# Kept activations, early residual loads and more buffers around two batch norms

## Chip, cores, metric

One core of a Trainium2 chip. The metric is the device time of one execution in microseconds (us). The record calls a run of one core slow when it is over 1.5% above the fastest of its kernel. The profile's own span is 1 to 3 us shorter than the timed runs, and single executions of one kernel differ by about 0.3%, mostly by where the first pass ends. So I read small differences not from whole times but from a point inside the profile: **E, the end of the last matmul of the second product**, and the time from E to the end of the span.

## The reference, cut

x has 128 batches of 128 nodes with 256 features. Four graph layers follow, each `x = x + layer(relu(layernorm(x)))`. Layers 0 to 2 are local to a batch. Layer 3 has two batch norms over all 16384 tokens:

```python
agg = einsum('nm,bmd->bnd', A_hat, features).reshape(-1, 256)
h   = relu(batchnorm(agg @ W1.T + b1))        # 512 wide: statistics over all tokens
out = batchnorm(h @ W2.T + b2)                # 256 wide: statistics over all tokens
return x3 + out                               # x3: the input of layer 3
```

Each batch norm needs every token before it can scale the first one. So there are three passes over the 32 groups of four batches: z = agg W1 + b1 (with x3 and z put aside), then O = relu(norm(z)) W2, then out = x3 + norm(O).

## The kernel before

z of a group is 1 MB, x3 and the output are 512 KB each. The first pass stores z and x3 to DRAM. O stays in SBUF (128 KB per partition). The parts concerned:

```python
        # end of the first pass, for a group g
        nc.gpsimd.dma_start(X3[g], xt)
        # ... z[:, j, :] = bw1T.T @ gT + b1, its bn_stats ...
        nc.sync.dma_start(Z[g], z)

    sc1, sh1 = bn_affine(stats1, FC, g1_c, be1_c, "bn1")     # the root runs on GpSimd
    # ... O[g] allocated ...
    with tc.tile_pool(name="passB", bufs=4) as wb:           # second product
        for g in range(NG):
            z = wb.tile([P, FC, T], FP, tag="z", name=f"zi_{g}")
            nc.sync.dma_start(z, Z[g])
            # relu(scale * z + shift) on ScalarE, 8 matmuls on TensorE,
            # bias and statistics on VectorE -> O[g], stats2

    sc2, sh2 = bn_affine(stats2, DC, g2_c, be2_c, "bn2")
    with tc.tile_pool(name="passC", bufs=3) as wc:           # last pass
        for g in range(NG):
            x3 = wc.tile([P, G, D], FP, tag="x3", name=f"x3i_{g}")
            nc.sync.dma_start(x3, X3[g])
            # O[g] scaled on ScalarE, turned by TensorE, added into x3 on VectorE
            nc.gpsimd.dma_start(out[g * G : (g + 1) * G].rearrange("b n d -> n b d"), x3)
```

Of the kernel before, what the change touches and what calls it, by code (L numbers as in the profile page):

```python
# [8 lines left out]
FP = mybir.dt.float32  # L9
# [13 lines left out]
def kernel(  # L23
# [25 lines left out]
):  # L49
    """Four pre-norm graph layers over x[b, n, d], node n on the partitions.  # L50

    Layers 0 to 2 and the first product of layer 3 are local to a batch and run
    as one pass over groups of G batches. Layer 3's two batch norms are over all
    tokens: its first product goes to DRAM with the residual, and comes back
    once its statistics are known; the second product stays on chip until its own
    statistics are.

    A mixing matrix A enters as A^T[m, n]. With activations h[m, d] as the
    stationary operand, the product is (A h)^T, which is what the next weight
    product contracts; so mixing also transposes. A (h W) is computed as (A h) W  # L60
    where A h is the smaller one.
    """
    nc = tc.nc
# [17 lines left out]
    def bank(shape, name):  # L81
        return psum.tile(shape, FP, tag="bank", name=name)
# [6 lines left out]
    adj_sb = const.tile([P, P], FP, name="adj_sb")  # L89
    nc.sync.dma_start(adj_sb, adj)  # L90

    passA = ExitStack()
# [44 lines left out]
    def inv_sqrt(dst, src, eps):  # L137
        """dst = 1 / sqrt(src + eps), a few numbers in each partition."""
        if eps:
            nc.vector.tensor_scalar(dst, src, eps, None, ALU.add)  # L140
            src = dst
        nc.gpsimd.tensor_tensor(dst, src, nhalf[:, : dst.shape[1]], ALU.pow)  # L142

    with tc.tile_pool(name="prep", bufs=1) as prep:

        def turned(dst, src, nr, name):
            """dst[p, c, r * P + q] = src[q, r, c * P + p]: the transpose of the
            matrix whose P-row blocks are src[:, r, :]."""
            ncol = src.shape[-1] // P
            for c in range(ncol):  # L150
                pt = bank([P, nr, P], f"{name}_{c}")
                for r in range(nr):
                    nc.tensor.transpose(pt[:, r, :], src[:, r, c * P : (c + 1) * P], ident)
                nc.vector.tensor_copy(dst[:, c, :].rearrange("p (r q) -> p r q", r=nr), pt)
# [4 lines left out]

        # layer 0: origin * adj and origin^T * adj, origin = adj where adj <= 0, else 1  # L160
        for dst, src, name in ((ainT, adjT, "fi"), (aoutT, adj_sb, "fo")):
# [23 lines left out]

        # layer 1: the causal mask over the adjacency, Wq Wk^T and Wv Wo
        nc.gpsimd.affine_select(
# [17 lines left out]

        # layer 2: adj * adj
        nc.vector.tensor_tensor(a2T, adjT, adjT, ALU.mult)

        # layer 3: D^-1/2 (adj + I) D^-1/2 and what is used transposed
        an = prep.tile([P, P], FP, name="an")  # L210
# [33 lines left out]
    def norm(g, layer):  # L244
        """relu(layernorm(x)) of a group."""
        xt = X[g]
        st = small.tile([P, G, 6], FP, tag="st", name=f"st{layer}_{g}")
        mv = small.tile([P, G, 2], FP, tag="mv", name=f"mv{layer}_{g}")
        for b in range(G):
            nc.vector.bn_stats(st[:, b, :], xt[:, b, :])  # L250
        for b in range(G):
            nc.vector.bn_aggr(mv[:, b, :], st[:, b, :])
        rs = small.tile([P, G], FP, tag="rs", name=f"rs{layer}_{g}")
        inv_sqrt(rs, mv[:, :, 1], LN_EPS)
        sh = small.tile([P, G], FP, tag="sh", name=f"sh{layer}_{g}")
        nc.vector.scalar_tensor_tensor(sh, mv[:, :, 0], -1.0, rs, ALU.mult, ALU.mult)  # L256
        h = w.tile([P, G, D], FP, tag="h", name=f"h{layer}_{g}", bufs=3)
        for b in range(G):
            nc.scalar.activation(  # L259
                h[:, b, :], xt[:, b, :], AF.Relu, bias=sh[:, b : b + 1], scale=rs[:, b : b + 1]  # L260
            )
        return h

    def mixed(dst, src, aT, name):
        """dst[d, c, (b n)] = (A src[:, b, :])^T, chunks c of P features."""
        for c in range(src.shape[-1] // P):
# [7 lines left out]
    def front(g):  # L274
        """Layers 0 and 1 of a group of batches, in X[g]."""
        if g + 1 < NG:
# [4 lines left out]
        gl = small.tile([P, G, 3], FP, tag="gl", name=f"gl_{g}")  # L281
        gs = w.tile([P, D], FP, tag="gs", name=f"gs_{g}")
        for b in range(G):
# [60 lines left out]
        for b in range(G):  # L344
            for c in range(DC):
# [3 lines left out]
                )  # L349
        p = w.tile([P, G, P], FP, tag="p", name=f"p_{g}")  # L350
        nc.vector.scalar_tensor_tensor(
# [14 lines left out]
        for b in range(G):  # L366
            nc.tensor.transpose(pp[:, b, :], p[:, b, :], ident)
        pT = w.tile([P, G, P], FP, tag="pT", name=f"pT_{g}")
        nc.vector.tensor_copy(pT, pp)
# [13 lines left out]
    def back(g):  # L383
        """Layer 2 of a group, and layer 3 as far as its first product."""
        xt = X[g]
# [14 lines left out]
        yield  # L400
        uT = w.tile([P, HC1, T], FP, tag="hT", name=f"uT_{g}", bufs=3)
        mixed(uT, u, a2T, f"pmu_{g}")
# [38 lines left out]
        yield  # L441
        z = w.tile([P, FC, T], FP, tag="hT", name=f"zo_{g}", bufs=3)
        for j in range(FC):
# [7 lines left out]
            nc.vector.bn_stats(stats1[:, j, g, :], z[:, j, :])  # L451
        nc.sync.dma_start(Z[g], z)
        yield

    def together(*parts):
        """Emit parts in turns, a stage of each at a time."""
        parts = list(parts)
        while parts:
            parts = [q for q in parts if next(q, parts) is not parts]
# [6 lines left out]
    def bn_affine(stats, nch, gam, bet, name):  # L466
        """The scale and shift of a batch norm, a channel in each partition."""
        mv = const.tile([P, nch, 2], FP, name=f"mv_{name}")
# [9 lines left out]

    # layer 3: relu of the first batch norm, the second product kept on chip
    sc1, sh1 = bn_affine(stats1, FC, g1_c, be1_c, "bn1")  # L480
    keep = ctx.enter_context(tc.tile_pool(name="keep", bufs=1))
    O = [keep.tile([P, DC, T], FP, name=f"o_{g}") for g in range(NG)]
    with tc.tile_pool(name="passB", bufs=4) as wb:
        for g in range(NG):
            z = wb.tile([P, FC, T], FP, tag="z", name=f"zi_{g}")
            nc.sync.dma_start(z, Z[g])
            for j in range(FC):
                nc.scalar.activation(  # L488
                    z[:, j, :], z[:, j, :], AF.Relu,
                    bias=sh1[:, j : j + 1], scale=sc1[:, j : j + 1],  # L490
                )
            for i in range(DC):
                po = bank([P, T], f"po_{g}_{i}")
                for j in range(FC):
                    nc.tensor.matmul(  # L495
                        po, bw2T[:, j, i * P : (i + 1) * P], z[:, j, :],
                        start=(j == 0), stop=(j == FC - 1),
                    )
                nc.vector.tensor_scalar(O[g][:, i, :], po, b2_c[:, i : i + 1], None, ALU.add)
                nc.vector.bn_stats(stats2[:, i, g, :], O[g][:, i, :])  # L500

    # the second batch norm, turned back to node rows, and the residual
    sc2, sh2 = bn_affine(stats2, DC, g2_c, be2_c, "bn2")
    with tc.tile_pool(name="passC", bufs=3) as wc:
        for g in range(NG):
            x3 = wc.tile([P, G, D], FP, tag="x3", name=f"x3i_{g}")
            nc.sync.dma_start(x3, X3[g])
            for i in range(DC):
                nc.scalar.activation(
                    O[g][:, i, :], O[g][:, i, :], AF.Identity,  # L510
                    bias=sh2[:, i : i + 1], scale=sc2[:, i : i + 1],
                )
            for q in range(G // 2):
                pt = bank([P, 2, D], f"pto_{g}_{q}")
                for r in range(2):
                    b = 2 * q + r
                    for i in range(DC):
                        nc.tensor.transpose(
                            pt[:, r, i * P : (i + 1) * P], O[g][:, i, b * P : (b + 1) * P], ident
                        )  # L520
                nc.vector.tensor_tensor(
                    x3[:, 2 * q : 2 * q + 2, :], pt, x3[:, 2 * q : 2 * q + 2, :], ALU.add
                )
            nc.gpsimd.dma_start(
                out[g * G : (g + 1) * G].rearrange("b n d -> n b d"), x3
            )

# [33 lines left out]
```

## Time and profile before

Median 3216.8 us (4 runs, 3216.28 to 3217.32).

| stretch (us) | what | TensorE busy | DMA share |
|---|---|---|---|
| 0 to 2857 | first pass | 94% between 60 and 2840 | 0.06 |
| 2857 to 2867.2 | first batch norm's scale and shift, first z load | 0 | 0.72 |
| 2867.2 to 3088.8 | second product | all of it | 0.40 |
| 3088.8 to 3096.5 | second batch norm's scale and shift | little | 0.54 |
| 3096.5 to 3216 | last pass | 46% | 0.80 |

A busy engine is the bound only where it leaves no holes: TensorE in the first three rows but for one hole, nothing in the last.

### The profile page before, as it was taken

How to read it: one execution, taken by the hardware profiler on the slowest of the kernel's cores; microseconds unless marked ns; L12 is line 12 of the kernel's file. 1: busy time of each engine (PE TensorE's matmuls, PEld its weight loads, DVE VectorE, ACT ScalarE, POOL GpSimd, SP SyncE). 2: the span in 40 equal slices, each digit the busy share in tenths (PEclk: the TensorE clock that was granted, in tenths of full speed). 3: DMA queues.
4: the chain of work that ended last, by engine and by line, in shares of the span. 5: the costliest groups of instructions: out<-in, count | busy, mean ns of one | idle time of the engine just before them, and what ended most of it. 6: DMA issues, size and time to landing. Idle time of an engine off the chain costs nothing.

```text
span 3215.9 us, 27252 instructions
## 1 busy us (share of the span) xinstructions
PE 2936.7 (91%) x10287; PEld 1781.6 (55%) x10287; DVE 1329.0 (41%) x3629; ACT 945.1 (29%) x1765; POOL 176.5 (5%) x204
## 2 busy tenths in 40 slices
PE   5999999999999999999999999999999999989973
PEld 3555655555555555555555555555555555544443
DVE  5433344444443443344444443443344444224443
ACT  2222233323223222233323223222233322134460
POOL 0000000000000000000000000000000000000011
PEclk8999999999999999999999999999999999989975
DMA  2000000000000000000000000000000000024457
GB/s 101 27 14 20 20 27 27 27 27 27 26 27 27 27 14 20 20 27 27 27 27 27 27 27 27 26 14 21 19 26 27 27 27 20 20 111 149 152 181 263
DMA packets 44438, 142.45 MB, mean 44 GB/s; under 512 B 3586, under 2 KB 22548, under 8 KB 36116
## 3 DMA queue, kind: packets, MB, share of 16 engines
q1 hardware_dynamic: 33248, 105.46, 9.3%
q0 software_dynamic: 9216, 33.56, 2.7%
q8 instruction: 80, 1.31, 0.2%
q10 hardware_dynamic: 1844, 1.71, 0.2%
q14 instruction: 50, 0.41, 0.0%
HBM read 73.61 MB, written 67.11 MB: 44 GB/s over the span
## 4 chain that ended last, share of the span: by engine, by line
PE 60%; DVE 20%; issue 9%; ACT 4%; DMA 3%; POOL 3%; POOLq 0%; DVEq 0%; ACTq 0%; SPq 0%
PE p L408 17%; PE p L423 14%; PE pu L395 7%; DVE st L250 4%; ACT h L259 4%; PE pmu L269 4%; PE pq L326 4%; PE pv L337 3%; DVE gs L285 3%; POOL rs L142 3%; DVE stats L451 2%; DMA x3i<-x 2%; PE ps L346 2%; PE py L375 2%; PE pm_in L298 2%
## 5 line engine op out<-in xcount | busy, mean ns | idle before, releaser
L408 PE MATMUL p<-uT,w 128*128 128x512 f32 x2048 | 913.1, 592 | 0.0
L408 PEld LDWEIGHTS p<-uT,w 128*128 128x128 f32 x2048 | 379.4, 190 | 412.5 <-issue 394.4
L423 PE MATMUL p<-w,h2T 128*128 128x256 f32 x2048 | 447.2, 379 | 0.0
L423 PEld LDWEIGHTS p<-w,h2T 128*128 128x128 f32 x2048 | 389.1, 190 | 66.6 <-issue 15.3
L259 ACT ACTIVATE h<-x,sh,rs 128x256 f32<-128x256 f32 x512 | 265.5, 589 | 354.6 <-DVE sh L256 337.7
L269 PE MATMUL pg<-ahT,h 128*128 128x128 f32 x512 | 124.2, 435 | 146.5 <-ACT h L259 146.5
L446 PE MATMUL pz<-gT,bw1T 128*128 128x512 f32 x512 | 246.0, 629 | 4.0 <-DVE gT L272 3.6
L415 ACT ACTIVATE h2T<-p 128x512 f32<-128x512 f32 x128 | 75.7, 592 | 571.0 <-PE p L408 571.0
L395 PE MATMUL pu<-w,mT 128*128 128x512 f32 x512 | 228.8, 600 | 14.0 <-DVE mT L272 14.0
L413 DVE TENSOR_SCALAR h2T<-p 128x512 f32<-128x512 f32 x128 | 88.3, 690 | 365.1 <-PE p L408 365.1
L495 PE MATMUL po<-zi,bw2T 128*128 128x512 f32 x512 | 221.6, 596 | 10.5 <-ACT zi L488 10.5
L432 DVE TENSOR_TENSOR x<-pr,x 128x512 f32<-128x512 f32 x64 | 43.7, 683 | 447.4 <-PE pr L431 447.4
L269 PEld LDWEIGHTS pg<-ahT,h 128*128 128x128 f32 x512 | 115.7, 317 | 173.1 <-ACT h L259 173.0
L427 ACT COPY s<-p 128x512 f32<-128x512 f32 x64 | 37.5, 586 | 567.6 <-PE p L423 567.6
L250 DVE BATCH_NORM_STATS2 st<-x 128x6 f32<-128x256 f32 x512 | 190.8, 413 | 4.2 <-DMA x<-in_x_dram 2.0
L142 POOL TENSOR_TENSOR rs<-rs,nhalf 128x4 f32<-128x4 f32 x128 | 129.8, 1014 | 1135.7 <-DVE rs L140 1135.7
L495 PEld LDWEIGHTS po<-zi,bw2T 128*128 128x128 f32 x512 | 97.8, 191 | 134.3 <-issue 112.9
L446 PEld LDWEIGHTS pz<-gT,bw1T 128*128 128x128 f32 x512 | 98.9, 203 | 129.1 <-issue 92.9
L285 DVE SCALAR_TENSOR_TENSOR gs<-h,gw 128x256 f32<-128x256 f32 x384 | 161.4, 420 | 15.9 <-ACT h L259 0.7
L395 PEld LDWEIGHTS pu<-w,mT 128*128 128x128 f32 x512 | 94.9, 190 | 127.5 <-issue 90.4
L299 DVE TENSOR_TENSOR m_in<-pm_in,eb 128x512 f32<-128x512 f32 x64 | 44.3, 692 | 234.9 <-PE pm_in L298 234.9
L488 ACT ACTIVATE zi<-zi,sh_bn,sc_bn 128x512 f32<-128x512 f32 x128 | 93.4, 802 | 118.4 <-DMA zi<-z 118.4
(116 smaller groups left out, 2931.5 us busy)
## 6 DMA issues: line engine op xcount, KB each, us to landing
z<-zo SPq DMA_DIRECT2D x32, 1024.0 KB, 3.9
zi<-z SPq DMA_DIRECT2D x32, 1024.0 KB, 4.8
x<-in_x_dram SPq DMA_DIRECT2D x32, 512.0 KB, 5.9
x<-x POOLq DMA_DIRECT2D x32, 512.0 KB, 3.0
x3i<-x SPq DMA_DIRECT2D x32, 512.0 KB, 5.1
out_dram<-x3i POOLq DMA_DIRECT2D x32, 512.0 KB, 4.6
w<-in_L_gnn_W_dram SPq DMA_DIRECT2D x1, 2048.0 KB, 11.6
bw<-in_L_gnn_W_dram ACTq DMA_DIRECT2D x2, 512.0 KB
```

The lines of the kernel that those rows point to most:

```text
L142: nc.gpsimd.tensor_tensor(dst, src, nhalf[:, : dst.shape[1]], ALU.pow)
L250: nc.vector.bn_stats(st[:, b, :], xt[:, b, :])
L259: nc.scalar.activation(h[:, b, :], xt[:, b, :], AF.Relu, bias=sh[:, b : b + 1], scale=rs[:, b : b + 1])
L269: nc.tensor.matmul(pm[:, b, :], src[:, b, c * P : (c + 1) * P], aT, start=True, stop=True)
L285: nc.vector.scalar_tensor_tensor(gs, h[:, b, :], 1.0, gw[:, i, :], ALU.mult, ALU.mult, accum_out=gl[:, b, i : i + 1],)
L326: nc.tensor.matmul(pq, m_qk[:, c, i * P : (i + 1) * P], hT[:, c, :], start=(c == 0), stop=(c == DC - 1),)
L337: nc.tensor.matmul(pv[:, r, :], hT[:, c, b * P : (b + 1) * P], w_vo[:, c, :], start=(c == 0), stop=(c == DC - 1),)
L395: nc.tensor.matmul(pu, mT[:, c, b * P : (b + 1) * P], w1[:, c, :], start=(c == 0), stop=(c == DC - 1),)
L408: nc.tensor.matmul(p2, w2[:, c, j * P : (j + 1) * P], uT[:, c, :], start=(c == 0), stop=(c == HC1 - 1),)
L423: nc.tensor.matmul(p3[:, r, :], h2T[:, j, b * P : (b + 1) * P], w3[:, j, :], start=(j == 0), stop=(j == HC2 - 1),)
L446: nc.tensor.matmul(pz, bw1T[:, c, j * P : (j + 1) * P], gT[:, c, :], start=(c == 0), stop=(c == DC - 1),)
L495: nc.tensor.matmul(po, bw2T[:, j, i * P : (i + 1) * P], z[:, j, :], start=(j == 0), stop=(j == FC - 1),)
```

## The change

Its intent is threefold. The second product begins with the three groups whose z was made last, which are kept in SBUF. Six x3 loads are made during the second product, and nine more into the space of the z buffers, so that 15 x3 buffers are in use instead of three. Loads go to GpSimd's queue, and the output leaves in half groups on SyncE's queue. To find room, some buffers of the first pass are halved. The core of the diff:

```diff
+    zp = zs.enter_context(tc.tile_pool(name="zp", bufs=3, side="right"))
+    KEPT = range(NG - 3, NG)
...
-        z = w.tile([P, FC, T], FP, tag="hT", name=f"zo_{g}", bufs=3)
+        z = ZT[g] = zp.tile([P, FC, T], FP, tag="z", name=f"zo_{g}")
...
-        nc.sync.dma_start(Z[g], z)
+        if g not in KEPT:
+            nc.sync.dma_start(Z[g], z)
...  (gs, p, pT: bufs=1; uT: bufs=2)
+    EARLY = 6
+    x3p = ctx.enter_context(tc.tile_pool(name="x3p", bufs=EARLY, reuse_waits="tile"))
+    zin = zs.enter_context(tc.tile_pool(name="zin", bufs=2, side="right", reuse_waits="tile"))
+    ORDER = [*KEPT, *(g for g in range(NG) if g not in KEPT)]
...
-        for g in range(NG):                      # second product
-            z = wb.tile(...); nc.sync.dma_start(z, Z[g])
+    for n, g in enumerate(ORDER):
+        z = ZT[g]
...
+        if n + 5 < NG:
+            load_z(n + 5)
+        if n % 4 == 3 and n // 4 < EARLY:
+            load_x3(n // 4, x3p, "x3")           # nc.gpsimd.dma_start
+    zs.close()
+    late = ctx.enter_context(tc.tile_pool(name="late", bufs=9, reuse_waits="tile"))
+    for g in range(EARLY, EARLY + 9):
+        load_later(g)
     sc2, sh2 = bn_affine(stats2, DC, g2_c, be2_c, "bn2")
...
-            nc.gpsimd.dma_start(out[g * G : (g + 1) * G].rearrange("b n d -> n b d"), x3)
+            at = g * G + 2 * q                   # inside the loop over halves q
+            nc.sync.dma_start(out[at : at + 2].rearrange("b n d -> n b d"), x3[:, half, :])
+        if g + EARLY + 9 < NG:
+            load_later(g + EARLY + 9)
```

More of the change, by code (lines that the diff above doesn't have):

```diff
@@ L90 @@
     nc.sync.dma_start(adj_sb, adj)
+    zs = ExitStack()
+    zp = zs.enter_context(tc.tile_pool(name="zp", bufs=3, side="right"))
+    KEPT = range(NG - 3, NG)
+    ZT = {}
     passA = ExitStack()
@@ L281, in front @@
         gl = small.tile([P, G, 3], FP, tag="gl", name=f"gl_{g}")
-        gs = w.tile([P, D], FP, tag="gs", name=f"gs_{g}")
+        gs = w.tile([P, D], FP, tag="gs", name=f"gs_{g}", bufs=1)
         for b in range(G):
@@ L349, in front @@
                 )
-        p = w.tile([P, G, P], FP, tag="p", name=f"p_{g}")
+        p = w.tile([P, G, P], FP, tag="p", name=f"p_{g}", bufs=1)
         nc.vector.scalar_tensor_tensor(
@@ L367, in front @@
             nc.tensor.transpose(pp[:, b, :], p[:, b, :], ident)
-        pT = w.tile([P, G, P], FP, tag="pT", name=f"pT_{g}")
+        pT = w.tile([P, G, P], FP, tag="pT", name=f"pT_{g}", bufs=1)
         nc.vector.tensor_copy(pT, pp)
@@ L400, in back @@
         yield
-        uT = w.tile([P, HC1, T], FP, tag="hT", name=f"uT_{g}", bufs=3)
+        uT = w.tile([P, HC1, T], FP, tag="hT", name=f"uT_{g}", bufs=2)
         mixed(uT, u, a2T, f"pmu_{g}")
@@ L477, in bn_affine @@
         return sc, sh
-    sc1, sh1 = bn_affine(stats1, FC, g1_c, be1_c, "bn1")
-    keep = ctx.enter_context(tc.tile_pool(name="keep", bufs=1))
-    O = [keep.tile([P, DC, T], FP, name=f"o_{g}") for g in range(NG)]
-    with tc.tile_pool(name="passB", bufs=4) as wb:
-        for g in range(NG):
-            z = wb.tile([P, FC, T], FP, tag="z", name=f"zi_{g}")
-            nc.sync.dma_start(z, Z[g])
+    keep = ctx.enter_context(tc.tile_pool(name="keep", bufs=1, reuse_waits="tile"))
+    O = [keep.tile([P, DC, T], FP, name=f"o_{g}") for g in range(NG)]
@@ new lines, with load_z @@
+    EARLY = 6
+    x3p = ctx.enter_context(tc.tile_pool(name="x3p", bufs=EARLY, reuse_waits="tile"))
+    zin = zs.enter_context(tc.tile_pool(name="zin", bufs=2, side="right", reuse_waits="tile"))
+    ORDER = [*KEPT, *(g for g in range(NG) if g not in KEPT)]
+    R = {}
+    def load_z(n):
+        g = ORDER[n]
+        m = n - len(KEPT)
+        pool, tag = (zin, "zi") if m < 2 or m % 5 >= 3 else (zp, "z")
+        ZT[g] = pool.tile([P, FC, T], FP, tag=tag, name=f"zi_{g}")
+        nc.sync.dma_start(ZT[g], Z[g])
@@ new lines, in load_x3 @@
+    def load_x3(g, pool, tag):
+        R[g] = pool.tile([P, G, D], FP, tag=tag, name=f"x3i_{g}")
+        nc.gpsimd.dma_start(R[g], X3[g])
+    load_z(3)
+    load_z(4)
+    sc1, sh1 = bn_affine(stats1, FC, g1_c, be1_c, "bn1")
+    for n, g in enumerate(ORDER):
+        z = ZT[g]
+        for j in range(FC):
+            nc.scalar.activation(
+                z[:, j, :], z[:, j, :], AF.Relu,
+                bias=sh1[:, j : j + 1], scale=sc1[:, j : j + 1],
+            )
+        for i in range(DC):
+            po = bank([P, T], f"po_{g}_{i}")
@@ L487 @@
             for j in range(FC):
-                nc.scalar.activation(
-                    z[:, j, :], z[:, j, :], AF.Relu,
-                    bias=sh1[:, j : j + 1], scale=sc1[:, j : j + 1],
-                )
-            for i in range(DC):
-                po = bank([P, T], f"po_{g}_{i}")
-                for j in range(FC):
-                    nc.tensor.matmul(
-                        po, bw2T[:, j, i * P : (i + 1) * P], z[:, j, :],
-                        start=(j == 0), stop=(j == FC - 1),
-                    )
-                nc.vector.tensor_scalar(O[g][:, i, :], po, b2_c[:, i : i + 1], None, ALU.add)
-                nc.vector.bn_stats(stats2[:, i, g, :], O[g][:, i, :])
@@ L503 @@
-    sc2, sh2 = bn_affine(stats2, DC, g2_c, be2_c, "bn2")
-    with tc.tile_pool(name="passC", bufs=3) as wc:
-        for g in range(NG):
-            x3 = wc.tile([P, G, D], FP, tag="x3", name=f"x3i_{g}")
-            nc.sync.dma_start(x3, X3[g])
-            for i in range(DC):
-                nc.scalar.activation(
-                    O[g][:, i, :], O[g][:, i, :], AF.Identity,
-                    bias=sh2[:, i : i + 1], scale=sc2[:, i : i + 1],
-                )
-            for q in range(G // 2):
-                pt = bank([P, 2, D], f"pto_{g}_{q}")
-                for r in range(2):
-                    b = 2 * q + r
-                    for i in range(DC):
-                        nc.tensor.transpose(
-                            pt[:, r, i * P : (i + 1) * P], O[g][:, i, b * P : (b + 1) * P], ident
-                        )
-                nc.vector.tensor_tensor(
-                    x3[:, 2 * q : 2 * q + 2, :], pt, x3[:, 2 * q : 2 * q + 2, :], ALU.add
-                )
-            nc.gpsimd.dma_start(
-                out[g * G : (g + 1) * G].rearrange("b n d -> n b d"), x3
-            )
+                nc.tensor.matmul(
+                    po, bw2T[:, j, i * P : (i + 1) * P], z[:, j, :],
+                    start=(j == 0), stop=(j == FC - 1),
+                )
@@ new lines, with load_later @@
+            nc.vector.tensor_scalar(O[g][:, i, :], po, b2_c[:, i : i + 1], None, ALU.add)
+            nc.vector.bn_stats(stats2[:, i, g, :], O[g][:, i, :])
+        if n + 5 < NG:
[4 more added lines that the diff above has]
+    late = ctx.enter_context(tc.tile_pool(name="late", bufs=9, reuse_waits="tile"))
+    def load_later(g):
+        load_x3(g, *((late, "x3l") if EARLY <= g < EARLY + 9 or g % 5 > 1 else (x3p, "x3")))
@@ new lines @@
+    for g in range(EARLY, EARLY + 9):
+        load_later(g)
+    sc2, sh2 = bn_affine(stats2, DC, g2_c, be2_c, "bn2")
+    for g in range(NG):
+        x3 = R[g]
+        for i in range(DC):
+            nc.scalar.activation(
+                O[g][:, i, :], O[g][:, i, :], AF.Identity,
+                bias=sh2[:, i : i + 1], scale=sc2[:, i : i + 1],
+            )
+        for q in range(G // 2):
+            pt = bank([P, 2, D], f"pto_{g}_{q}")
+            for r in range(2):
+                b = 2 * q + r
+                for i in range(DC):
+                    nc.tensor.transpose(
+                        pt[:, r, i * P : (i + 1) * P], O[g][:, i, b * P : (b + 1) * P], ident
+                    )
+            half = slice(2 * q, 2 * q + 2)
+            nc.vector.tensor_tensor(x3[:, half, :], pt, x3[:, half, :], ALU.add)
+            at = g * G + 2 * q
+            nc.sync.dma_start(out[at : at + 2].rearrange("b n d -> n b d"), x3[:, half, :])
+        if g + EARLY + 9 < NG:
+            load_later(g + EARLY + 9)
```

## The prediction

> **What bounds the kernel now.** I read the page first for the shape of the run: TensorE is busy 91% of 3215.9 us, but the last slices are unlike the rest.
>
> ```profile
> PE   5999999999999999999999999999999999989973
> DMA  2000000000000000000000000000000000024457
> GB/s 101 27 14 20 20 27 27 27 27 27 26 27 27 27 14 20 20 27 27 27 27 27 27 27 27 26 14 21 19 26 27 27 27 20 20 111 149 152 181 263
> ```
>
> A slice is 80 us. For 34 slices TensorE is at nine tenths and the DMA engines nearly idle; at the end TensorE falls and the traffic rises tenfold. Next I cut the run into stretches at the borders that the timeline shows: the first pass (layers 0 to 3's first product) ends near 2857 us, the second product runs from 2867.2 to 3088.8, the last pass from there to the end. The columns are length, busy us (and instructions) of TensorE, its weight loads, VectorE, ScalarE and GpSimd, then the granted clock, the DMA share and GB/s.
>
> ```profile
> 60.00:2840.00 2780.00, 2613.24 (x9376) 1608.32 (x9375) 1151.83 (x3310) 786.61 (x1533) 145.22 (x156) 0.97 0.06 24
> 2857.00:2867.20 10.20, 0.01 (x1) 0.01 (x1) 2.78 (x7) 1.25 (x3) 1.01 (x1) 0.66 0.72 276
> 2867.20:3088.80 221.60, 221.60 (x512) 97.81 (x512) 92.22 (x127) 92.56 (x127) 0.00 (x0) 0.99 0.40 144
> 3088.80:3096.50 7.70, 2.64 (x12) 2.17 (x12) 4.07 (x9) 3.51 (x5) 0.70 (x1) 0.73 0.54 204
> 3096.50:3216.00 119.50, 55.13 (x247) 45.33 (x245) 40.47 (x63) 41.71 (x60) 24.21 (x32) 0.54 0.80 268
> ```
>
> So the first pass is TensorE's (94% busy). Between it and the second product there is a hole of 10.2 us without a matmul. In the second product TensorE is busy for all of 221.6 us: the waits of ScalarE for z in that stretch (118.4 us in total) cost nothing. In the last pass no compute engine is busy for half of the time and the DMA engines are, at 0.80. The list of waits for the last stretch and the chain agree: VectorE, which adds the residual, waits for x3, and the queue that loads x3 waits for the store that has to empty one of three buffers.
>
> ```profile
> SPq L507 <- DMA out_dram<-x3i: 104.7, 29, 11.2
> DVE x3i L521 <- DMA x3i<-x: 73.2, 29, 6.2
> ```
>
> ```profile
> 2858.14 1.03 DVE mv_bn L470
> 2859.20 0.18 DVE sc_bn L140
> 2859.44 1.01 POOL sc_bn L142
> ...
> 3101.41 4.82 DMA x3i<-x
> ...
> 3107.94 4.17 DMA out_dram<-x3i
> 3112.16 4.16 DMA x3i<-x
> ```
>
> The first three lines are the statistics of the first batch norm, which no change to the loads can remove; the others show a store and a load taking turns on the path, because three buffers do not hold enough in flight.
>
> **What the Trainium skill says.** (1) "DMA: Bandwidth & Descriptors", section "Issuing engines are not separate DMA queues": transfers started by any engine run on the same 16 DMA engines, and a second issuer only saves issue time. So exchanging the queues (loads to GpSimd, stores to SyncE) should be worth nothing in bandwidth. The trace fits: with both queues at work in 3120 to 3200 us the DMA share is 0.85 and 284 GB/s move, below the 351 GB/s that SyncE's z loads alone reach at a share of 0.94 from 2862 to 2868. (2) Same page, "Anatomy of one DMA — SWDGE (gpsimd) path": a transfer costs about 2.0 us fixed plus bytes / 436 GB/s. For 512 KB that is 3.2 us; the trace has 3.0 us for the x3 stores of the first pass when nothing else moves, and 5.1 and 4.6 us for loads and stores in the last pass. The fixed part is latency, so more buffers hide it. (3) Same page, "Where 436 GB/s comes from": 435 GB/s is the ceiling of the ports. The z store between 1032 and 1042 us moves 1.05 MB at 25.6% of 10 us, that is 410 GB/s of full share; so this sets the least time. (4) "TensorE: Matmul & The Clock Gate", Part 1: after an idle window of about 3.4 us the clock drops to half. The trace shows granted clock 0.50 in 2861 to 2869 us and again in 3120 to 3200.
>
> **The change part by part.**
>
> *Buffers of the first pass.* gs, p and pT go from two buffers to one, uT from three shared with z to two of its own, z gets three. Each is rewritten only a whole group (some 87 us) later, long after its reader. Cost 0; I allow plus or minus 3 us for another order of instructions.
>
> *Second pass starts on kept z.* Before, the last matmul of the first pass ended near 2856.65. ScalarE, VectorE and GpSimd then work out scale and shift until 2861.05. ScalarE's first relu starts only at 2866.32, when the first z (issued at 2861.48) has landed, and the first matmul at 2867.19. With group 29's z in SBUF the relu can start at 2861.1, takes 0.80, and the first matmul comes at about 2862.0. Gain 5.2 us. The hole is still 5.3 us, longer than the clock's window, so the first four or so matmuls are at half clock as they are now: no gain there. Three z stores and three z loads of 1 MB vanish, but all of them lie under TensorE's work: 0.
>
> *Second product.* 512 matmuls at 0.43 us = 220 us on TensorE, unchanged. Six x3 loads (3 MB) are added to a stretch at DMA share 0.40: hidden, 0. Its end, E, moves from 3088.8 to 3083.6.
>
> *Last pass.* Before: 32 loads and 32 stores of 512 KB after E, 33.5 MB in about 125 us. After: six loads are done by E, so 26 loads and 32 stores, 30.4 MB. Nine of the 26 are issued about at E on GpSimd's queue into space that the z buffers leave. I work out the lower tile's place by adding up sizes: it overlaps the buffer of the very last group, so I do not expect these nine to get ahead of E. With 15 buffers and no turn-taking I expect the DMA engines to be full from E + 1 us to the last store.
> Busy time of one load: three x3 loads in 3088 to 3097 take 46.1% of 9 us = 4.15 us, so 1.38 each. One store: a store of 4 KB packets alone is 0.16 x 8 us = 1.28 (window 2842 to 2850). But SyncE's queue splits rows of 1 KB: the x load of the first pass is 528 packets and takes 17.6% of 10 us = 1.76 us for the same bytes. [...]I take 1.6 for two halves, an estimate between the two.
> 26 x 1.38 + 32 x 1.6 = 35.9 + 51.2 = 87.1 us. Loads and stores in each other's way cost more: in 3120 to 3200 us 0.85 x 80 = 68 us of DMA time moved 22.7 MB, 21.7 pairs, 3.1 us a pair where the parts alone are 1.38 + 1.28 = 2.66, a factor of 1.17. Part of that is latency at the start of lone transfers, which deep queues hide, so I charge half of it to the 17 pairs that really mix: 17 x 2.98 x 0.085 = 4.3. Sum 91.4 us; at a share of 0.97, 94.2. With 1 us to start and 1.8 us for the last receipt: E + 97 = 3180.6.
>
> *The second batch norm's chain.* Its reciprocal root runs on GpSimd, in whose queue nine loads now stand before it. An issue of such a contiguous load should cost what the x3 store's does, 0.594 us, so nine take 5.4 us and the root starts some 3 us later than now (now 2.9 us after E). VectorE's first add then comes near E + 10 rather than E + 6.7. The nine loads keep the DMA engines full for 12 us, so this is hidden; I add 0.
>
> *Compute in the last pass.* ScalarE 2 x 0.71 = 1.41 us a group, VectorE 2 x 0.65 = 1.3, TensorE 8 transposes in 1.94 at half clock (1.15 at full). 32 x 1.94 + 10 = E + 72 at worst, under E + 97: not the bound.
>
> Sum: 5.2 us from the start, about 30 us from the last pass (124.4 from E to the end of the work before, 97 after, gives 28 to 30 with the slack of the last store). On the clock of the timed runs, which is 1 us above the profile's span: **3181 us**, 1.1% less.
>
> **Rivals.**
> (a) *Turn-taking was not the cost; loads and stores on HBM limit each other at 284 GB/s.* For it: the 0.85 share leaves only 15% idle. Against: z loads and single transfers run at 351 to 410. Then 30.4 MB take 107 us: 3193.
> (b) *Half stores of 1 KB rows are dear.* At the x load's 1.76 us per 512 KB, 32 x 0.16 = 5 us more, some 3186; and 64 completions instead of 32. Against: they queue up back to back.
> (c) *DMA engines reach the ceiling* seen alone (410 GB/s for loads, 1.47 us per store): 26 x 1.28 + 32 x 1.47 = 80 us, about 3168. Compute would then be near the bound if TensorE stays at half clock.
> (d) *GpSimd's nine loads hold the root for longer*, waiting for a z buffer or for their issue, and the DMA engines run dry: 5 to 10 us more, 3186 to 3191.
> (e) *The nine loads get ahead of E*, because buffers of earlier groups come free first: up to nine loads hidden, 12 us less, about 3169.
>
> **Range and chances.** 2% is 64 us. Even with no limit from DMA, compute ends near E + 72 = 3156, so "faster by over 2%" needs more than compute allows. Slower needs a new wait of 64 us, for which nothing speaks. The range runs from (c) or (e) to (a): 3167 to 3194. Chances: faster 0.02, same 0.97, slower 0.01.
>
> **What would show it.** Right: first matmul of the second product near 2862 and TensorE full for 221 us after it; six x3 loads inside that stretch; DMA share of 0.95 or more and about 320 GB/s from E on; loads over well before stores; VectorE waiting for x3 little in the first 15 groups; the root on GpSimd starting 5 us or more after E. Wrong: a share that stays near 0.85, a gap in DMA after E, a first pass longer or shorter by over 3 us, or stores in 1 KB packets of well over 50 ns.

## The result

3169.78 us median (3168.76 to 3170.8, 4 runs) beside 3216.82 us before: ratio 0.9852, 95% interval 0.9838 to 0.9866. Ratios here are the mean time of one kernel's fast runs over that of the other's fast runs of the same rounds, so not quite the ratio of the two medians. The prediction said 3181 in a range of 3167 to 3194, so the time lies inside it, 11 us below its centre.

The busy slices of the changed kernel, to be laid beside those of before:

```profile
PE   5999999999999999999999999999999999999995
DMA  2000000000000000000000000000000000004429
GB/s 102 15 25 14 27 27 27 27 27 27 27 27 14 20 21 27 27 27 27 27 27 27 14 21 20 27 27 27 27 27 27 27 22 12 2 39 158 147 104 374
```

There is now a single slice in which the DMA engines are at nine tenths, and it carries 374 GB/s. The stretches of the changed kernel (length, busy us and instructions of TensorE, weight loads, VectorE, ScalarE, GpSimd, then clock, DMA share, GB/s):

```profile
2857.00:2861.90 4.90, 0.00 (x1) 0.00 (x1) 2.71 (x7) 1.17 (x3) 2.52 (x4) 0.82 0.04 10
2861.90:3084.40 222.50, 222.50 (x512) 98.14 (x512) 92.09 (x127) 92.35 (x127) 0.64 (x2) 0.99 0.38 137
3084.40:3093.70 9.30, 1.69 (x8) 1.28 (x8) 3.17 (x8) 2.56 (x4) 5.41 (x10) 0.74 0.78 281
3093.70:3167.90 74.20, 38.30 (x251) 29.96 (x249) 40.53 (x64) 42.70 (x61) 9.02 (x17) 0.80 1.03 375
```

The hole ahead of the second product shrank from 10.2 to 4.9 us. The product takes 222.5 us as against 221.6. From E to the end it was 127.1 us before and is 83.5 us now (the last two rows give 9.3 + 74.2). The DMA share is at 1.03: packets overlap in this count, even those of a single queue (104.8% in a line under e4), so a full set of engines can show a little over 1. The waits of VectorE for x3, 73.2 us in 29 waits before, have become one of 8.5 us. It is at group 17 (34 of the 64 additions come before it), one of those whose buffer a store had to empty first:

```profile
POOL x3i L504 <- DVE x3i L556: 30.8, 11, 11.7
POOL x3i L504 <- DMA out_dram<-x3i: 12.2, 6, 5.0
DVE x3i L556 <- DMA x3i<-x: 8.5, 1, 8.5
```

GpSimd, which now issues the loads, still waits for stores. While it does, the DMA engines stay full (share 1.05 to 1.07 in every 10 us from 3100 to 3160), so these waits leave no DMA time unused. The GpSimd timeline after E (start us, us, instruction, and the idle time before it) shows the nine loads and the root behind them:

```profile
3084.94 0.53 POOL L504 DMA_DIRECT2D x3i<-x  x1 [222.40 <-PE po L519]
3085.62 4.16 POOL L504 DMA_DIRECT2D x3i<-x  x8 [0.16 <-issue]
3089.80 0.72 POOL L147 TENSOR_TENSOR sc_bn<-sc_bn,nhalf 128x2 f32<-128x2 f32 x1
```

The six early loads were not spread over the second product, as their place in the program suggests. Their source line (first and last start) and GpSimd's timeline show when they were issued:

```profile
L504 POOL DMA_DIRECT2D x3i<-x x32: 527/527/600, 2844.4 to 3142.0; - x32
2860.38 2.16 POOL L504 DMA_DIRECT2D x3i<-x  x4
```

Two went out at 2844.4, still in the first pass, and four at 2860.4, just before the product began. Their buffers were free, so a place later in the program did not hold them back; what stood before the four in GpSimd's queue was the first root (2859.4 us).

### The profile page after: what moved, and what is told of

Read it like the earlier page. It is cut to its first block, busy times and chain, and to the rows that moved or that the text cites. A ratio compares the mean times of both kernels' runs of the same rounds, so it can differ in the third digit from the quotient of the medians.

```text
span 3167.9 us, 27265 instructions
## 1 busy us (share of the span) xinstructions
PE 2919.7 (92%) x10287; PEld 1764.8 (56%) x10287; DVE 1328.0 (42%) x3629; ACT 944.7 (30%) x1765; POOL 169.2 (5%) x204
## 4 chain that ended last, share of the span: by engine, by line
PE 68%; DVE 20%; ACT 5%; POOL 3%; issue 2%; DMA 2%; POOLq 0%; ACTq 0%; DVEq 0%; SPq 0%
PE p L413 18%; PE p L428 14%; PE pu L400 7%; PE po L519 7%; DVE st L255 4%; ACT h L264 4%; PE pmu L274 4%; PE pq L331 4%; PE pv L342 3%; DVE gs L290 3%; POOL rs L147 3%; DVE stats L456 2%; PE py L380 2%; PE ps L351 2%; PE pm_in L303 2%
## 5 line engine op out<-in xcount | busy, mean ns | idle before, releaser
L519 PE MATMUL po<-zi,bw2T 128*128 128x512 f32 x464 | 199.3, 592 | 0.0
L519 PEld LDWEIGHTS po<-zi,bw2T 128*128 128x128 f32 x464 | 88.2, 190 | 111.0 <-issue 104.3
L274 PEld LDWEIGHTS pmu<-a2T,u 128*128 128x128 f32 x1024 | 119.4, 192 | 15.3 <-issue 15.3
```

The lines of the kernel that those rows point to most:

```text
L274: nc.tensor.matmul(pm[:, b, :], src[:, b, c * P : (c + 1) * P], aT, start=True, stop=True)
L519: nc.tensor.matmul(po, bw2T[:, j, i * P : (i + 1) * P], z[:, j, :], start=(j == 0), stop=(j == FC - 1),)
```

## The experiments

Times are medians. Beside each stands the ratio to the kernel before in the same rounds, and the time from E to the end of the profile, which is free of the first pass's scatter. The first four ran with before at 3217.6 us, the next four with before at 3217.6, the last three with before at 3216.2.

| run | us | ratio (95%) | from E to the end |
|---|---|---|---|
| before | 3216.8 | | 127.1 |
| changed | 3169.8 | 0.9852 (0.9838 to 0.9866) | 83.5 |
| e1 kept z only | 3211.4 | 0.9982 (0.9967 to 0.9997) | 124.2 |
| e2 15 buffers only | 3176.7 | 0.9874 (0.9860 to 0.9889) | 87.4 |
| e3 no early x3 | 3177.3 | 0.9876 (0.9861 to 0.9891) | 91.3 |
| e4 queues as before | 3167.0 | 0.9843 (0.9827 to 0.9859) | 81.2 |
| a1 changed again | 3170.0 | 0.9851 (0.9837 to 0.9864) | 83.2 |
| e5 whole stores | 3168.7 | 0.9849 (0.9836 to 0.9863) | 82.3 |
| e7 nine loads on SyncE | 3168.0 | 0.9846 (0.9832 to 0.9859) | 82.6 |
| e8 more hidden | 3164.9 | 0.9837 (0.9823 to 0.9850) | 78.5 |
| e9 fifteen hidden | 3161.3 | 0.9826 (0.9811 to 0.9841) | 78.1 |
| e10 six buffers | 3181.7 | 0.9887 (0.9870 to 0.9903) | 91.9 |
| e11 four buffers | 3201.2 | 0.9948 (0.9933 to 0.9963) | 110.1 |

All outputs are right.

### e1: the kept z alone

```diff
 # the changed kernel, with the last pass of the kernel before
-    x3p, late, load_later, half stores
+    with tc.tile_pool(name="passC", bufs=3) as wc: ...
```

> Second pass of the changed kernel (kept z first), last pass of the kernel before (three x3 buffers, loads on SyncE, whole stores on GpSimd, no early x3). Theory: the start of the second product gains the 5.3 us between 2867.19 and 2861.90 and nothing else moves: 3211.5 us. Rival (the start is swallowed by a later wait, or other orders of instructions matter): 3216 or off by over 3 us.

Measured 3211.4 us. The time is as expected, but the profile shows that it is made of two other parts. The product starts 5.3 us sooner and ends only 4.4 us sooner, because in this execution more of its first matmuls ran at the low clock. The first 8 us of the product, before and in this change (the changed kernel's row serves, the start is the same), with the clock in the third column from the right:

```profile
2867.20:2875.20 8.00, 8.00 (x15) 3.58 (x16) 1.45 (x2) 7.75 (x12) 0.00 (x0) 0.79 0.73 306
```

```profile
2861.90:2869.90 8.00, 8.00 (x13) 3.52 (x14) 1.45 (x2) 8.00 (x12) 0.64 (x2) 0.68 0.69 258
```

The mean clock of this stretch fell from 0.79 to 0.68, and two matmuls fewer fit in it: 2 x 0.43 = 0.9 us. That is not an effect of the shorter hole, as far as the runs show. Of the other kernels with a hole of 10.5 to 10.6 us, e10 shows 0.78 in its first 8 us and a product of 221.7 us, but e2 and e11 show 0.62 and 223.0 us; with the hole of 5.3 us all runs have products of 222.2 to 222.5 us. How many matmuls stay slow differs from one execution to the next, and the profile of before happened to have few. And the last pass of this run gained 2.9 us (124.2 against 127.1) because its first three x3 loads were already issued at 2856.7 us, as their buffers do not lie under the z buffers here.

### e2: one number, 15 buffers instead of three

```diff
-    with tc.tile_pool(name="passC", bufs=3) as wc:
+    with tc.tile_pool(name="passC", bufs=15) as wc:
```

> The kernel before with one number changed: 15 instead of 3 x3 buffers in the last pass. Theory (taking turns was the cost; all packets stay 4 KB): 32 x 1.27 + 32 x 1.30 = 82 us of DMA work at a full share, 4 us at the two ends, so the work ends 86 us after TensorE's last product instead of 127: 3176 us. Rival (a) of the prediction (reads and writes on HBM limit each other at 284 GB/s): no change, 3217. Rival (the six early loads and the exchange of queues carry the gain): above 3200.

Measured 3176.7 us. This is the disputed point of the prediction, and rival (a) falls. Reads and writes together do not limit each other at 284 GB/s; the same 64 transfers as before, from the same queues, run at 414 GB/s once enough of them are in flight. One number gives 40.9 us (3217.6 - 3176.7), where the whole change gives 47.0 us beside before in its own rounds (3216.8 - 3169.8).

The share of 0.86 before made the room look smaller than it was. The queue lines from 3100 to 3160 us (packets, MB, share), loads on q1 and stores on q0, of before:

```profile
q1 hardware_dynamic: 2304, 8.39, 45.5%
q0 software_dynamic: 2423, 8.81, 40.5%
```

and of e2:

```profile
q1 hardware_dynamic: 3360, 12.20, 50.4%
q0 software_dynamic: 3467, 12.63, 51.9%
```

A packet of a load took 190 ns on average before and 144 in e2 (45.5% of 16 x 60 us over 2304 packets, and the like), one of a store 160 and 144. A load and a store together cost 3.14 us of all engines before and 2.59 in e2, no more than the two alone (1.38 + 1.28, as the prediction measured them). So a part of the share of 0.86 was time that goes away when more transfers are in flight.

### e11 and e10: four and six buffers

> The kernel before with four x3 buffers. Theory: 11.1 / 4 = 2.78 us a group, just above the DMA engines' 2.57: 32 x 2.78 + 9 = 98 us after the last product, 3188 us; up to 3195 if latencies grow with load. Rival (HBM or the kind of queue limits): 3210 or more.

> The kernel before with six x3 buffers instead of three. Theory (turn-taking): three buffers at 3.7 us a group make a round of 11.1 us for one buffer; six of them would allow 1.85 us a group, less than the 2.57 us that a load and a store take of the DMA engines, so the engines are the bound and six do as well as 15: 3177 to 3180 us. Rival (in-flight bytes help steadily, as latencies grow with load): 3190 or more.

Measured 3201.2 and 3181.7 us. The edit is that of e2 with 4 and 6. The stretch from 3100 to 3160 us with three, four, six and 15 buffers, one fence each:

```profile
3100.00:3160.00 60.00, 32.22 (x147) 26.13 (x145) 19.76 (x32) 38.21 (x55) 12.06 (x16) 0.58 0.86 287
```

```profile
3100.00:3160.00 60.00, 30.01 (x160) 25.04 (x161) 22.57 (x36) 38.27 (x55) 13.36 (x18) 0.73 0.94 325
```

```profile
3100.00:3160.00 60.00, 45.34 (x209) 32.67 (x206) 29.55 (x47) 37.91 (x54) 18.06 (x24) 0.66 1.01 392
```

```profile
3100.00:3160.00 60.00, 43.45 (x206) 30.75 (x206) 32.80 (x51) 35.32 (x51) 19.17 (x27) 0.68 1.02 414
```

287, 325, 392, 414 GB/s: the number of buffers, and with it the bytes that can be in flight, makes the rate. My arithmetic of rounds was too simple. Divided evenly, four buffers should have reached 2.78 us a group; at 325 GB/s a group's 1.05 MB takes 3.2 us. A round of one buffer got longer with more of them (median landing of loads and stores 5.6 and 4.5 us with three, 6.3 and 5.6 with four, 6.4 and 7.5 with six). So the rival "in-flight bytes help steadily" has the better part at four buffers, and at six, with a share of 1.01, the theory does: the rest to 15 buffers is 4.5 us from E to the end.

### e3: the six early x3 loads held back

```diff
-        if n % 4 == 3 and n // 4 < EARLY:
-            load_x3(n // 4, x3p, "x3")
...
+    for g in range(EARLY):
+        R[g] = x3p.tile([P, G, D], FP, tag="x3", name=f"x3i_{g}")
+        nc.scalar.copy(R[g][:, 0, 0:1], O[ORDER[-1]][:, 1, 0:1])   # holds it until the product is done
+        nc.sync.dma_start(R[g], X3[g])
```

> The changed kernel, but the six early x3 loads are held until the second product is done (a copy of one number from its last result into each tile first) and issued on SyncE. Theory (from there on the DMA engines are the bound): 6 x 1.28 = 7.7 us more, 3177.5 us. Rival (the first store and compute set the end, the loads were hidden anyway): 3170, no change.

Measured 3177.3 us; from E to the end 91.3 us against 83.5, so 7.8 us for six loads, 1.3 us each. Past E the time is set by DMA work, and what is taken out of it is gained in full.

### e4: queues as before

```diff
-        nc.gpsimd.dma_start(R[g], X3[g])
+        nc.sync.dma_start(R[g], X3[g])
...
-            nc.sync.dma_start(out[at : at + 2].rearrange("b n d -> n b d"), x3[:, half, :])
+        nc.gpsimd.dma_start(out[g * G : (g + 1) * G].rearrange("b n d -> n b d"), x3)
```

> The changed kernel with the queues exchanged back: x3 loads on SyncE, whole-group stores on GpSimd, so stores are again 4 KB packets. Theory (DMA-bound; 4 packets of 1 KB at 46 ns against one of 4 KB at 159 to 162 ns): 32 x (1.48 - 1.28) = 6.4 us less, 3163.5 us; the root on GpSimd is no longer behind nine loads but that is hidden. Rival (half stores on SyncE are part of the gain, as they start sooner): slower than the changed kernel, 3173 or more.

Measured 3167.0 us, 81.2 us from E to the end against 83.5: 2.3 us less, not 6.4, in whole times 2.8 us with overlapping intervals. So the exchange of queues in the change did not help; by the profile it and the half stores together cost 2 to 3 us. One part is in the packets. The queue line of a late stretch of the changed kernel (packets, MB, share), in which stores run alone:

```profile
q1 hardware_dynamic: 3711, 3.58, 104.8%
```

3.58 MB in 3711 packets are 1 KB rows, at 358 GB/s. In the mixed stretch from 3110 to 3140 us the 1 KB stores of the changed kernel and the 4 KB stores of e4 compare as follows:

```profile
3110.00:3140.00 30.00, 22.44 (x145) 17.74 (x144) 18.89 (x31) 26.40 (x38) 5.81 (x11) 0.89 1.06 396
```

```profile
3110.00:3140.00 30.00, 20.88 (x124) 15.31 (x123) 16.13 (x26) 24.41 (x35) 9.71 (x14) 0.84 1.02 409
```

396 against 409 GB/s is 3%, where packet times alone (46 ns for 1 KB, 159 for 4 KB) had let me expect more. The share of 1.06 against 1.02 fits small packets that overlap more in this count. The mixed stretch lasts some 50 us, so 3% are about 1.6 us, an estimate. The edit also undoes the half stores and takes the nine loads out of the root's way; e5 and e7 do one of these each and show 1.2 and 0.9 us less than the changed kernel, neither clear of noise. So the 2.3 us can't be put down to the packets alone.

### e5 and e7: whole stores; nine loads out of the root's way

```diff
 # e5: one store a group on SyncE
-            nc.sync.dma_start(out[at : at + 2].rearrange("b n d -> n b d"), x3[:, half, :])
+        nc.sync.dma_start(out[g * G : (g + 1) * G].rearrange("b n d -> n b d"), x3)
 # e7: only the nine loads after the product on SyncE
-        load_later(g)
+        R[g] = late.tile([P, G, D], FP, tag="x3l", name=f"x3i_{g}")
+        nc.sync.dma_start(R[g], X3[g])
```

> The changed kernel as it is, on the chip of the three runs beside it: 3170 us. It is there to have differences of 2 to 3 us against runs of the same rounds.

> The changed kernel with one store of 512 KB per group on SyncE's queue instead of two of 256 KB; packets stay 1 KB. Theory (only bytes and packets count in a full queue): within 1 us of the changed kernel. Rival (half stores get the first bytes out sooner and buffers free sooner): 2 us or more slower. Rival (64 completions cost): 1 to 2 us faster.

> The changed kernel with the nine x3 loads after the second product issued on SyncE, so that the reciprocal root on GpSimd is not behind them (it should start 2.9 instead of 5.4 us after the last product, and the first store 2.5 us sooner). Theory (hidden, the DMA engines are busy with the nine loads): within 1 us of the changed kernel. Rival (the chain of the second batch norm is on the path): 2.5 us faster.

The changed kernel gave 3170.0 beside them, e5 3168.7 and e7 3168.0; from E to the end 83.2, 82.3 and 82.6 us. In e7 the root does start 2.9 us after E instead of 5.4, and the first transpose comes 5.1 instead of 7.6 us after E, yet of those 2.5 us no more than 0.6 to 0.9 arrive at the end of the profile (the medians differ by 2.0 us, with overlapping intervals). The wait was all but hidden behind loads, as predicted. Halving the stores gave nothing either; whole ones are 1 us better if anything, which these runs do not separate from noise.

### e8 and e9: the better version, and its limit

```diff
 # e8: e4, and
-    EARLY = 6
+    EARLY = 8; LATE = 8
-    zin = ...tile_pool(name="zin", bufs=2, ...)
+    zin = ...tile_pool(name="zin", bufs=1, ...)
-        pool, tag = (zin, "zi") if m < 2 or m % 5 >= 3 else (zp, "z")
+        pool, tag = (zin, "zi") if n in (3, 7, 11, 15, 19, 22, 25, 28) else (zp, "z")
 # e9: further, LATE = 9, two 0.5 KB constants moved out of the way, and
+        pool, tag = (zin, "zi") if n in (3, 6, 9, 12, 15, 19, 23, 27, 31) else (zp, "z")
```

> Loads on SyncE and whole stores on GpSimd (4 KB packets), eight x3 loads early instead of six, four z buffers instead of five, and the last groups' z placed so that the buffers in the way of the eight later loads come free before the end of the second product. Theory (from the last product on, DMA work sets the end, so whatever moves ahead of it is gained at 1.27 us a load): if six of the eight get ahead, 8 loads less than the run with queues as before, about 3158 us; if the buffers lie otherwise than I think, two less, 3164.5. Rival (compute and first store set the end by now): 3166 or more.

> As the run with more hidden loads, but with nine later buffers moved by 1 KB so that each lies in one z buffer, and the last groups' z placed so that these come free in the order in which the loads stand in the queue: 15 of 32 x3 loads should land before the end of the second product instead of nine. Theory: after the first store (9.6 us after the last product) 15 loads and 32 stores are left, 24.6 MB at 414 GB/s = 59.5 us, end near E + 70: 3158 us. Rival (the start of the stores or compute at 1.41 us a group holds the end by now): 3163 or more.

e8 gave 3164.9 us, 5.1 us better than the changed kernel in the same rounds; only one of the eight later loads got ahead of E, the second stood behind the last group's z buffer. So the first estimate of the layout was wrong, and the time is the one expected for that case. In e9 seven got ahead, so 15 loads in all were done by E. It gave 3161.3 us, ratio 0.9826, the lowest of all runs, but its interval overlaps that of e8, they ran beside different runs of before, and from E to the end the two are equal. Here are 9.6 us after E and then the rest, e8 first:

```profile
3084.60:3094.20 9.60, 4.54 (x21) 4.09 (x21) 5.70 (x11) 5.42 (x8) 1.51 (x2) 0.73 0.91 347
3094.20:3163.10 68.90, 34.10 (x238) 25.71 (x236) 38.47 (x61) 39.84 (x57) 23.34 (x31) 0.80 0.97 371
```

```profile
3080.20:3089.80 9.60, 4.54 (x21) 4.05 (x21) 5.68 (x11) 5.39 (x8) 1.51 (x2) 0.73 0.30 109
3089.80:3158.30 68.50, 33.99 (x238) 25.70 (x236) 38.47 (x61) 39.88 (x57) 23.34 (x31) 0.80 0.96 360
```

With 15 loads hidden the DMA engines have little to do until the first store (share 0.30 where e8 has 0.91), and what follows is as long in both, 68.5 and 68.9 us. The rival of e9 held: more hidden loads give nothing past e8. The count of buffers fits this: e8 has 16 and e9 has 17, so no more loads than these can be done before a first store is. At 1.3 us a load, e8's share of 0.91 is some seven loads after nine hidden ones and e9's 0.30 some two after 15, so both come to their limit, and about as many loads and all 32 stores are left. Neither a shorter way from E to the first store nor still more buffers was tried.

## Why the prediction was right, and where it was off

**Right.** *The bound of the last pass.* It was read from the list of waits as turn-taking of loads and stores over three buffers, with the DMA engines idle in between. e2 shows it: buffers alone give 40.9 us. *The start of the second product*: 2861.90 measured, 2862.0 predicted. *Hidden parts*: E at 3084.4 (3083.6 predicted), the six early loads invisible in the product (222.5 us with them, and 222.5 in e1 without), worth 7.8 us past E (e3). *The nine late loads not ahead of E*: the first was issued at 3084.94. *The root behind nine loads and that this costs nothing*: it started 5.4 us after E, and e7 gains at most 0.9 us without it. *Compute not the bound*: group 17's wait is the only one of VectorE for a load, and TensorE's clock was at 0.80, not 0.50, in the last pass. *No room for 2%*: the interval ends at 0.9838 on the fast side.

**Off: the terms of the last pass's sum.** I predicted E + 97 and the profile shows E + 83.5, so the centre was missed by more than the small error at E explains, though the time lies in the range. The queue lines from E to the end (3084.4 to 3167.9 us), stores on q1 and loads on q0:

```profile
q1 hardware_dynamic: 17408, 16.78, 57.9%
q0 software_dynamic: 3744, 13.63, 42.0%
```

| term (us) | predicted | measured |
|---|---|---|
| one load, 26 of them | 1.38 | 42.0% of 83.5 over 26: 1.35 |
| the stores of one group, 32 of them | 1.6 | 57.9% of 83.5 over 32: 1.51 |
| all of these | 87.1 | 83.4 |
| loads and stores in each other's way | 4.3 | none seen: a pair costs 2.59 in e2, and 2.66 alone |
| share under one, and the two ends | 2.8 + 2.8 | 0.1 in all, as the count runs to 1.07 where both mix |

The differences are 3.7, 4.3 and 5.5 us, 13.5 in all. The largest single step that failed is the surcharge for mixing. I measured a factor of 1.17 in the kernel before and took half of it for contention and half for latency at the start of lone transfers; with 15 buffers (e2) the same mixture ran at 414 GB/s and nothing of the factor was left. The rest are sizes: the store, and a share that I took as 0.97 at most. Rival (c), the ceiling seen alone, had 3168 and its cause is the nearest. Rival (e) had 3169, but the nine loads did not get ahead of E, so its number agrees by luck. One sum in the recorded text does not come out: its 124.4 us from E to the end less 97 are 27, not 28 to 30; from E to the end of the span it was 127.1, which gives the 30 that it uses. And of the 118.4 us of ScalarE's waits for z that are said to cost nothing, the first 8.9 us are the hole itself; the prediction counts the hole in another place.

**Off, smaller.** The kept z gave 4.4 us at E in these two profiles and not 5.2, which lies within the scatter of the clock (see e1). Of the six early loads, expected inside the product, two were issued before it and four at its start. And the exchange of queues, which the prediction charged at 32 x (1.6 - 1.28) = 10 us as part of the change, cost 2 to 3 us in e4, half stores included. It had also taken from a shared set of engines that the exchange is worth nothing in bandwidth; mixed, the two ways differ by 3%.

**Open.** Why drains of stores alone run at 356 to 364 GB/s (e9 and the changed kernel, with packets of 4 KB and of 1 KB) while mixtures reach 395 to 414. In such drains the size of the packets makes no clear difference (358 and 356 GB/s), in mixtures it does. It is measured here, its cause is not.

## What to carry to other kernels

When a load waits for a store and the DMA engines are below a share of one, give the ring more buffers first; here that one number gave 41 us where the whole change gave 47, and the rate of two alternating transfers measured with a small ring is no limit of the memory. Past that point count DMA work: each load moved ahead of the bound's start was gained in full (1.3 us each in e3), until the first store found the engines idle (e9). Look at the packets that a queue makes before you exchange queues; here the exchange gained nothing.

## What the Trainium skill lacked or had wrong

- "DMA: Bandwidth & Descriptors", section "Issuing engines are not separate DMA queues": the engines are shared, as it says, but the section does not say that the packets can change with the queue chosen (other sections of the page treat packet sizes and an overhead per packet; none says what SyncE's queue makes of such rows). The same output went as 1 KB packets (46 ns) from SyncE's queue and as 4 KB packets (159 to 165 ns) from GpSimd's: 396 against 409 GB/s when mixed with loads, and no clear difference alone (358 and 356).
- Same page, "Where 436 GB/s comes from": it says that the HBM side, about 358 GB/s for one core, binds for transfers between HBM and SBUF, and also gives a measured 425. The runs here, with one core at work, show 414 GB/s for loads and stores together, so 358 did not bind there, and 356 to 364 for stores alone.
- Same page, "Anatomy of one DMA — SWDGE (gpsimd) path": 2.0 us plus bytes / 436 GB/s fits a lone store of 512 KB (3.2 us against 3.0). It does not say how many transfers in flight cover the fixed part: three buffers of 512 KB gave 287 GB/s, four 325, six 392, 15 gave 414.

On "TensorE: Matmul & The Clock Gate", Part 1, nothing was found wrong: it says that the clock's window runs freely, and here the mean clock of the first 8 us after the hole differed between executions whose holes were the same (0.62, 0.78 and 0.79 after 10.5 to 10.6 us).
